# Attention blocks of a twelve-stage kernel: rounding of the maxima and division by the sums moved to GpSimd, value products half a key tile later, causal masks by matmul

## The chip, the cores and the metric

The kernel runs on one core of one Trainium2 chip. The metric is device time in microseconds (us): 3737.1 us before, the median of three runs (3736.11 to 3738.52). The engines are named as in the profile: PE (TensorE matmul), PEld (its weight load), DVE (VectorE), ACT (ScalarE), POOL (GpSimd), SP (SyncE, which issues the DMAs).

## The reference

One sequence `x` of 2048 tokens with 128 channels passes through four layers of the form feed-forward, attention, feed-forward, each added to `x` after a layer norm:

```
x = x + 0.5 * ffn_L(layernorm(x))
x = x + attn_L(layernorm(x))
x = x + 0.5 * ffn_L(layernorm(x))        # L = 0, 1, 2, 3
```

The attentions are what matters here. Each computes `softmax(q k^T * scale) v` for every head and multiplies by an output matrix. Layer 0 has 8 heads of 16 channels and is causal, with a geometric term added to the scores. Layers 1 and 2 have 16 heads of 8 channels and are not causal; layer 1 adds a bias, layer 2 turns queries and keys (rope). Layer 3 is causal with 16 heads of 64 channels and latent values. The feed-forward layers (two with routing to experts, one with quantised weights, one with ternary weights) are not touched.

## The kernel before, in words

The kernel works through twelve stages in order. While one runs, the first steps of the next are woven into it by hand (`Stage.lead`). `x` lies in SBUF as four chunks of 512 tokens (`xs`); `NC` is 4, `TC` is 4 tiles of 128 tokens a chunk, `CH` is 512.

**Attention of layers 0, 1 and 2** is written by `packed` (L1325), which calls `flash` (L974). Four heads form a group. A *block* is one group with one chunk of queries: `its` (L1441 to L1444) lists 8 blocks in layer 0 (two groups, four chunks) and 16 in each of layers 1 and 2 (four groups, four chunks, the group changing slowest). Every block is worked in two passes.

- **Pass A** (`stream_a`, `some`) finds each query's largest score. PE makes the scores of two heads, 128 queries by 512 keys each, in a PSUM pair of banks (L1071; two such pairs exist, tag `s1`), and DVE reduces the pair to two columns (L1089). In layers 1 and 2 this is 32 pairs a block. In layer 0 the pairs on the diagonal (8 a block, 64 in all) are narrower, 128, 256, 384 or 512 keys, and need the causal mask: DVE adds a strip of the mask and takes the maximum in one custom instruction for each head, with a read of its accumulator behind each (L1079 to L1087). `maxima` (L1097) then reduces the four key chunks to `mx`, negated, and `put_max` (L1551) rounds it to bf16 on DVE (`top`, L1556) and keeps the remainder beside it (L1557). A later step `put` (L1561) adds both to the queries by matmuls into the bank `pm` and ACT copies the result to `q2`, so that the scores of pass B come out with the maximum subtracted. That step falls due 2000 units of a recording clock after `maxima` (L1107).
- **Pass B** (`stream_b`) makes the scores again, transposed, 128 keys by 512 queries for each head (L1213, three single banks, tag `s2`), ACT takes the exponential (L1222) into a tile `pt`, and PE multiplies `pt` with the values (L1159) into one held bank `pv`. A key tile has four heads. In layers 1 and 2 the value products of the last key tile are issued in two halves of 256 queries, after the second and the fourth head of the current one (`values`, L1130; call at L1236). In layer 0 POOL masks the diagonal `pt` tiles (L1224).
- **The end of a block** is `finish` (L1579): ACT copies `pv` to `ov`; `normal` (L1584) transposes it on PE into a bank `po` (L1587), where every head has its result and its sum of exponentials; DVE takes the reciprocal of the sums (L1592) and multiplies (L1593) into `os`. After the last group of a query chunk, `out_a` (L1604) transposes `os` on PE (L1607), ACT copies it, and `out_b` multiplies by the output matrix (L1615) and adds to `x` (L1620).

**Attention of layer 3** (`attn3`, L1793) also uses `flash`, with two heads a block (`nh == 2`, called `halved`). Its causal mask is added in PSUM by four small bf16 matmuls for each pair, made from halves of the identity and of the mask (`half_masks`, L1021 to L1028; the halves are loaded and cast at L1010 to L1019).

**What sets the order.** Passes A and B are two generators. The loop at L1272 to L1291 advances them so that A stays about one block ahead of B, and everything that PE does in both passes is recorded in that order (`keep_in_program_order`, through `pe`). A step such as `put`, `normal`, `out_a` or `out_b` is put on a list with a due time of the recording clock (`after`, L995) and is recorded into the same order when the clock passes it. The other engines are ordered by a scheduler; the reductions of pass A have high priority, and the first one of a block is tied behind the last operation of `put_max` (`newest`, L1061, L1101). Each engine runs its own list in order, so an instruction that waits holds up those behind it.

Of the kernel before, what the change touches and what calls it, by code (L numbers as in the profile page):

```python
# [64 lines left out]
def tile_macaron(ctx: ExitStack, tc: tile.TileContext, a: dict, out: bass.AP, stages=STAGES):  # L65
# [33 lines left out]
    nc.gpsimd.memset(minus_half, -0.5)  # L99

# [873 lines left out]
    def flash(io, pool, early, its, nh, causal, scale, s1, s2, pv_mm, put_max, begin, finish, poll=None,  # L974
# [8 lines left out]
        halved = nh == 2  # L983
        clock = [0.0]
        total = [0]
# [22 lines left out]
        if halved:  # L1008

            halves = {}  # L1010
            for name in ("ident", "maskq", "maskk"):
                raw = pool().tile([P, 2, P], F32, name="halfraw", tag="halfraw", bufs=2)
                for j in range(2):
                    nc.sync.dma_start(
                        out=raw[P // 2 * j : P // 2 * (j + 1)],
                        in_=a["consts"][:, slice(*CONSTS[name])].rearrange("(b i) k -> i b k", b=2),
                    )
                halves[name] = pool().tile([P, 2, P], BF16, name="half" + name)
                nc.vector.tensor_copy(halves[name], raw)  # L1019
# [9 lines left out]

        if tiled and causal:  # L1030
            junk = pool().tile([P, CH], F32, name="junk")
            strip = pool().tile([P, CH], F32, name="strip")
            nc.gpsimd.memset(strip[:, : CH - P], 0.0)
            nc.vector.tensor_copy(strip[:, CH - P :], cs("maskq"))
# [19 lines left out]
        def some(n, turns, mp):  # L1054

            g, qc = its[n]
            nk = chunks(qc)
            for first, (r, kcs) in enumerate(turns):
                before = hook(n, kcs[0], r) if hook is not None else None
                if first == 0 and before is None:  # L1060
                    before = newest[0]  # L1061
                for kc in kcs:
                    for j0 in range(0, nh, 2):
                        ps = first_pass_bank()
                        last = causal and kc == qc
                        masked = last and not tiled
                        w = (r + 1) * P if last else CH
                        for j in range(2):
                            o = j * CH
                            lhsT, rhs = s1(n, j0 + j, r, kc)  # L1070
                            pe(nc.tensor.matmul(  # L1071
                                ps[:, o : o + w], lhsT, rhs[:, :w], start=True, stop=not masked
                            ))
                            pos[0] += w
                        if masked:
                            half_masks([ps[:, j * CH + w - P : j * CH + w] for j in range(2)], "maskq")
                        both = ps.rearrange("p (j n) -> p j n", j=2)
                        with tc.high_priority() if not waiting[0] else nullcontext():
                            if last and tiled:  # L1079
                                for j in range(2):  # L1080
                                    ins = nc.vector.tensor_tensor_reduce(
                                        junk[:, :w], both[:, j, :w], strip[:, CH - w :], 1.0, NEG,
                                        ALU.add, ALU.max, mp[:, r, j0 + j, kc : kc + 1],
                                    )
                                    if before is not None:
                                        in_order(ins, before)
                                        before = None  # L1087
                            else:
                                ins = nc.vector.tensor_reduce(  # L1089
                                    mp[:, r, j0 : j0 + 2, kc], both[:, :, :w], AX.X, ALU.max,  # L1090
                                )
                        if before is not None:
                            in_order(ins, before)
                            before = None
                        yield 2 * w if tiled else w

        def maxima(n, mp):  # L1097
            nk = chunks(its[n][1])
            mx = pool().tile([P, TC, nh], F32, name="mx", tag="mxa", bufs=3)
            nc.vector.tensor_reduce(mx, mp[:, :, :, :nk], AX.X, ALU.max, negate=True)  # L1100
            put, newest[0] = put_max(n, mx, pe)  # L1101

            def done():
                put()
                ready.add(n)

            after(2000.0, done)  # L1107
# [19 lines left out]
        def stream_b():  # L1127
            pend = [None]

            def values(half=None):  # L1130

                if pend[0] is None:
                    return
                n, kt, nt, c0, pts, pv, last_exp = pend[0]
# [13 lines left out]
                if half == 0:  # L1148
                    pend_half[0] = 1
                    if hi == CH:  # L1150
                        pend[0] = None
                        pend_half[0] = 0
                else:
                    pend[0] = None
# [22 lines left out]
            for n, (g, qc) in enumerate(its):  # L1177
# [4 lines left out]
                pv = None  # L1182
                for kt in range(nt):
# [4 lines left out]
                    if halved:  # L1188
# [11 lines left out]
                        for j in range(2):  # L1200
                            pts[j] = early.tile([P, CH], F32, name="pt", tag="pt", bufs=2 * nh + 2)
# [4 lines left out]
                    for at_j, j in enumerate(() if halved else order):  # L1206
                        if alive[0] or at_j % 2:
# [13 lines left out]
                        pt = early.tile([P, CH], F32, name="pt", tag="pt", bufs=2 * nh + 2)  # L1221
# [12 lines left out]
                        if tiled and alive[0]:  # L1234
                            if at_j % 2:
                                values(at_j // 2)  # L1236
                        elif at_j == (split_at if alive[0] else nh - 1):
                            values()
                    if pv is None:
                        pv = held("pv")  # L1240
                    pend[0] = (n, kt, nt, c0, pts, pv, ex)
                    if not alive[0]:
                        io.lead(2.3)
                if poll is not None:
                    at[1] = nt
                    if flush and n + 1 < len(its) and its[n + 1][0] != g:
                        values()
                    poll(at)
            values()
# [72 lines left out]
    def attention_scratch(early):  # L1322
        return lambda dt, name: early.tile([P, CH], dt, name=name, tag="pt", bufs=10)

    def packed(io, early, hd, causal, scale, project, w, wv, wo, bias=None, outs=True):  # L1325
# [12 lines left out]
        scratch = attention_scratch(early)  # L1338
# [212 lines left out]
        def put_max(n, mx, pe):  # L1551
            top = tops[n % 3]
            tv = top.rearrange("p a r (j s) -> p a r j s", s=span)[:, :, :, :, 3:8:4]
            for i in range(nq):
                m = mx[:, :, i * per : (i + 1) * per]
                nc.vector.tensor_copy(tv[:, i, :, :, 0], m)  # L1556
                last = nc.vector.tensor_tensor(  # L1557
                    tv[:, i, :, :, 1], m, tv[:, i, :, :, 0], ALU.subtract
                )
# [19 lines left out]
        def finish(n, pv, after, pe):  # L1579
# [4 lines left out]
            def normal():  # L1584
                ps = bank("po")
                for r in range(TC):
# [3 lines left out]
                po = ps.rearrange("p (r j m) -> p r j m", r=TC, j=4)  # L1590
                rc = room[0].tile([P, TC, 4], F32, name="rc", tag="rc", bufs=2)
                nc.vector.reciprocal(rc, po[:, :, :, hd])  # L1592
                nc.vector.tensor_tensor(  # L1593
                    os[qc][:, :, g * 4 * hd : (g + 1) * 4 * hd].rearrange(
                        "p r (j d) -> p r j d", j=4
                    ),
                    po[:, :, :, :hd],
                    rc.unsqueeze(3).to_broadcast([P, TC, 4, hd]),
                    ALU.mult,
                )  # L1600
                if g == n_groups - 1:
# [62 lines left out]
        with tc.tile_pool(name="att", bufs=1) as pool, tc.tile_pool(name="far", bufs=1) as far:  # L1664
# [11 lines left out]
            room.append(far if causal else early if outs else pool)  # L1676
# [713 lines left out]
```

## Time and profile before

| what | value |
|---|---|
| median of the timed runs | 3737.1 us |
| the profiled execution's own time | 3720.8 us |
| its span in the trace | 3719.1 us |
| busy in the span | PE 3404.5 (92%), DVE 2853.9 (77%), ACT 2025.6 (54%), POOL 817.1 (22%) |
| granted PE clock, mean | 0.95 |
| attention of layer 0 | about 178 to 447 us |
| attention of layer 1 | about 855 to 1445 us |
| attention of layer 2 | about 1745 to 2345 us |
| attention of layer 3 | the stretch up to about 3570 us |

How to read it: a share of the span is an average over stages that are bound by different things. So the profile is asked by stage: windows of time for the busy engines, then the order of time around one block. The name of an operation gives the tile that it writes and those that it reads, its shapes and its count; "idle before" is the time for which its engine stood still just before, with the engine that ended this. A busy PE is not a PE at its peak, since the ends of overlapping matmuls are modelled.

### The profile page before, as it was taken

The page shows a single profiled execution, that of the slowest core. Times are in us where ns is not written, and L with a number is a line of the kernel's source. Part 1 is how long each engine was busy: PE and PEld are TensorE (multiplying, and loading weights), DVE is VectorE, ACT ScalarE, POOL GpSimd, SP SyncE. Part 2 cuts the span into 40 slices and gives each one's busy share as a digit, 9 for nine tenths or more (in the row PEclk, how much of TensorE's full clock was granted, in tenths as well). Part 3 has the DMA queues.
Part 4 walks back from the last instruction along what each step waited for, and adds up shares of the span by engine and source line. Part 5 has one row for each costly group of instructions (what it writes and reads, how often), then busy time and mean ns, then how long its engine had stood idle before and what let it go on. Part 6 is the DMA issues. An engine that isn't in the chain of part 4 may idle for free. (4 is left out here: it accounts for less than half of the span.)

```text
span 3719.1 us, 64518 instructions
## 1 busy us (share of the span) xinstructions
PE 3404.5 (92%) x25325; PEld 1837.3 (49%) x25325; DVE 2853.9 (77%) x4729; ACT 2025.6 (54%) x3815; POOL 817.1 (22%) x816
## 2 busy tenths in 40 slices
PE   7689987989999999997999999898889999999989
PEld 5543366854333333883333333376444444445457
DVE  6588556778999995778999999544777877788852
ACT  3346722317888888333888888731333344444442
POOL 1511124000000000210000000232555445533341
PEclk9779989979999999996999999898999999999999
DMA  3420123000000000100000000012443232211010
GB/s 106 98 52 14 37 62 91 7 20 9 15 6 16 6 4 7 55 25 21 10 16 10 12 6 1 26 44 68 151 146 112 96 106 98 97 57 52 24 35 12
DMA packets 124977, 170.18 MB, mean 46 GB/s; under 512 B 25152, under 2 KB 52930, under 8 KB 124672
## 3 DMA queue, kind: packets, MB, share of 16 engines
q1 hardware_dynamic: 122112, 160.80, 13.8%
q0 software_dynamic: 2560, 5.25, 0.9%
q8 instruction: 199, 3.26, 0.4%
q14 instruction: 106, 0.87, 0.1%
HBM read 101.25 MB, written 45.87 MB: 40 GB/s over the span
## 5 line engine op out<-in xcount | busy, mean ns | idle before, releaser
L1089 DVE TENSOR_REDUCE mp<-s 128x2 f32<-128x1024 f32 (+3 forms) x1440 | 1627.7, 1183 | 80.2 <-PE s L1071 56.7
L1222 ACT ACTIVATE pt<-s 128x512 f32<-128x512 f32 (+1 forms) x2368 | 1220.5, 601 | 217.7 <-PE s L1213 165.2
L1213 PE MATMUL s<-q,km 32*128 32x512 f32 (+2 forms) x2368 | 735.0, 493 | 28.8 <-ACT pt L1222 18.6
L1159 PE MATMUL pv<-pt,v 128*32 128x256 f32 (+1 forms) x8568 | 732.2, 414 | 22.9 <-ACT ov L1582 11.2
L1071 PE MATMUL s<-km,qt 32*128 32x512 f32 (+3 forms) x2368 | 617.1, 506 | 64.9 <-DVE mp L1089 45.3
L1213 PEld LDWEIGHTS s<-q,km 32*128 32x128 f32 (+1 forms) x2368 | 323.9, 184 | 531.4 <-issue 339.5
L1202 ACT ACTIVATE pt<-s 128x512 f32<-128x512 f32 (+3 forms) x640 | 306.3, 530 | 361.3 <-PE s L1194 216.3
L143 POOL TENSOR_TENSOR rs<-rs,minus_half 128x4 f32<-128x4 f32 x56 | 57.3, 1023 | 1491.8 <-DVE rs L142 1468.1
L2071 DVE TENSOR_TENSOR sum<-sum,pt 128x512 f32<-128x512 f32 (+3 forms) x328 | 260.0, 808 | 86.9 <-ACT pt L1202 85.6
L1159 PEld LDWEIGHTS pv<-pt,v 128*32 128x32 f32 x8568 | 169.2, 108 | 317.7 <-issue 147.1
L1194 PE MATMUL s<-q,k 64*128 64x512 f32 (+3 forms) x1920 | 295.1, 400 | 14.9 <-ACT pt L1202 10.5
L1159 PE MATMUL pv<-pt,latv 128*64 128x512 f32 (+3 forms) x1280 | 307.5, 560 | 1.3 <-ACT pt L1202 1.3
L2071 POOL TENSOR_TENSOR sum<-sum,pt 128x512 f32<-128x512 f32 (+1 forms) x200 | 264.7, 1324 | 179.8 <-ACT pt L1202 176.4
L1071 PEld LDWEIGHTS s<-km,qt 32*128 32x128 f32 (+1 forms) x2368 | 236.2, 191 | 123.8 <-DVE mp L1089 82.3
L1194 PEld LDWEIGHTS s<-q,k 64*128 64x128 f32 x1920 | 159.1, 186 | 222.8 <-issue 140.5
L715 ACT ACTIVATE sg<-pg 128x1024 f32<-128x1024 f32 x72 | 74.0, 1027 | 158.2 <-PE pg L229 142.0
L1071 PE MATMUL s<-k,q 64*128 64x512 f32 (+3 forms) x640 | 131.9, 430 | 19.0 <-DVE mp L1089 18.8
L1873 DVE TENSOR_TENSOR rot<-rot,tab 128x512 f32<-128x512 f32 x128 | 87.8, 686 | 74.8 <-PE rot L229 43.3
L725 PEld LDWEIGHTS pd<-l1d,h 128*128 128x128 f32 x1152 | 139.0, 191 | 5.6
L725 PE MATMUL pd<-l1d,h 128*128 128x128 f32 x1152 | 139.8, 275 | 0.0
L717 DVE TENSOR_TENSOR h<-pu,sg 128x1024 f32<-128x1024 f32 x72 | 87.8, 1220 | 51.7 <-PE pu L229 46.5
L1888 ACT CAST h<-rot 128x512 fp32r<-128x512 f32 x64 | 39.6, 619 | 159.5 <-POOL rot L1883 159.5
(572 smaller groups left out, 4736.3 us busy)
## 6 DMA issues: line engine op xcount, KB each, us to landing
tab<-in_l3rope SPq DMA_DIRECT2D x66, 256.0 KB
q<-q SPq DMA_DIRECT2D x32, 512.0 KB
k<-k SPq DMA_DIRECT2D x32, 512.0 KB
l0e<-in_l0e SPq DMA_DIRECT2D x32, 256.0 KB
q<-h SPq DMA_DIRECT2D x32, 256.0 KB
q<-rot SPq DMA_DIRECT2D x32, 256.0 KB
k<-h SPq DMA_DIRECT2D x32, 256.0 KB
k<-rot SPq DMA_DIRECT2D x32, 256.0 KB
```

The source lines that it names most:

```text
L715: nc.scalar.activation(sg, pg, AF.Silu)
L717: nc.vector.tensor_tensor(h.rearrange("p m n -> p (m n)"), pu, sg, ALU.mult)
L725: nc.tensor.matmul(pd[:, i, :], h[:, m, i * P : (i + 1) * P], wd[:, m, :], start=m == 0, stop=m == 1,)
L1071: pe(nc.tensor.matmul(ps[:, o : o + w], lhsT, rhs[:, :w], start=True, stop=not masked))
L1089: ins = nc.vector.tensor_reduce(mp[:, r, j0 : j0 + 2, kc], both[:, :, :w], AX.X, ALU.max,)
L1159: i = pe(nc.tensor.matmul(pv[out_rows, lo:hi], lhsT, pts[j][:, lo:hi], start=kt == 0, stop=kt == nt - 1 and hi == CH))
L1194: pe(nc.tensor.matmul(outs[j][:, c0:], lhsT, rhs[:, c0:], start=i == 0, stop=i == len(terms[0]) - 1 and not diag,))
L1202: ex = nc.scalar.activation(pts[j][:, c0:], outs[j][:, c0:], AF.Exp, scale=scale)
L1213: pe(nc.tensor.matmul(ps[:, c0:], lhsT, rhs[:, c0:], start=i == 0, stop=i == len(terms) - 1 and (tiled or not diag),))
L1222: ex = nc.scalar.activation(pt[:, c0:], ps[:, c0:], AF.Exp, scale=scale)
L1873: nc.vector.tensor_tensor(t.bitcast(F32), ps, halves["tabs"][i], ALU.mult)
L2071: eng.tensor_tensor(t[:, c0:], other[:, c0:], pts[j][:, c0:], ALU.add)
```

## The change

It has four parts, the first three of which concern layers 1 and 2 alone.

1. The rounding of the maxima (`put_max`) runs on GpSimd for every block but the first of a stage, and `put` falls due 3000 instead of 2000 units after `maxima`. The first reduction of the next block is tied behind `mx` itself.
2. The division: ACT copies `po` from PSUM to a tile `ot` in SBUF, and GpSimd raises the sums to the power -1 and multiplies. The last block of a stage keeps the old way on DVE.
3. The value products are issued half a key tile later; there are 12 `pt` tiles instead of 10, and the tiles of `ov` move to another pool.
4. Layer 0: the diagonal pairs of pass A get their mask by `half_masks`, as in layer 3, and then one plain reduction for both heads. The strip and the custom instruction are gone.

The diff, cut to its core:

```
+    minus_one = const.tile([P, TC, 4], F32, name="minus_one")
+    nc.gpsimd.memset(minus_one, -1.0)
...
+        lag = tiled and not causal
+        aside = tiled and not causal
...
-        if halved:
+        if causal:
             halves = {}
-            for name in ("ident", "maskq", "maskk"):
+            for name in ("ident", "maskq", "maskk")[: 3 if halved else 2]:
...
-        if tiled and causal:
-            junk = pool().tile([P, CH], F32, name="junk")
-            strip = pool().tile([P, CH], F32, name="strip")
...
-                        masked = last and not tiled
+                        masked = last
...
-                            if last and tiled:
-                                for j in range(2):
-                                    ins = nc.vector.tensor_tensor_reduce(
-                                        junk[:, :w], both[:, j, :w], strip[:, CH - w :], 1.0, NEG,
-                                        ALU.add, ALU.max, mp[:, r, j0 + j, kc : kc + 1],
-                                    )
...
-                            else:
-                                ins = nc.vector.tensor_reduce(
-                                    mp[:, r, j0 : j0 + 2, kc], both[:, :, :w], AX.X, ALU.max,
-                                )
+                            ins = nc.vector.tensor_reduce(
+                                mp[:, r, j0 : j0 + 2, kc], both[:, :, :w], AX.X, ALU.max,
+                            )
...
-            nc.vector.tensor_reduce(mx, mp[:, :, :, :nk], AX.X, ALU.max, negate=True)
-            put, newest[0] = put_max(n, mx, pe)
+            newest[0] = nc.vector.tensor_reduce(mx, mp[:, :, :, :nk], AX.X, ALU.max, negate=True)
+            if aside and n:
+                put, _ = put_max(n, mx, pe, nc.gpsimd)
+            else:
+                put, newest[0] = put_max(n, mx, pe)
...
-            after(2000.0, done)
+            after(3000.0 if aside and n else 2000.0, done)
...
-            pend = [None]
+            pend = []
...
+                        while not alive[0] and len(pend) > 1:
+                            values()
...
                         if tiled and alive[0]:
-                            if at_j % 2:
-                                values(at_j // 2)
+                            if at_j % 2 and (not lag or at_j == nh - 1 or len(pend) > 1):
+                                values(pend_half[0] if lag else at_j // 2)
...
                     if flush and n + 1 < len(its) and its[n + 1][0] != g:
-                        values()
+                        while pend:
+                            values()
...
-        def put_max(n, mx, pe):
+        def put_max(n, mx, pe, eng=nc.vector):
...
-                nc.vector.tensor_copy(tv[:, i, :, :, 0], m)
-                last = nc.vector.tensor_tensor(
-                    tv[:, i, :, :, 1], m, tv[:, i, :, :, 0], ALU.subtract
-                )
+                eng.tensor_copy(tv[:, i, :, :, 0], m)
+                last = eng.tensor_tensor(tv[:, i, :, :, 1], m, tv[:, i, :, :, 0], ALU.subtract)
...
+                if causal or n == len(its) - 1:
...
+                else:
+                    ot = room[1].tile([P, CH], F32, name="ot", tag="ov", bufs=2)
+                    nc.scalar.copy(ot, ps)
+                    po = ot.rearrange("p (r j m) -> p r j m", r=TC, j=4)
+                    rc = room[0].tile([P, TC, 4], F32, name="rc", tag="rc", bufs=2)
+                    nc.gpsimd.tensor_tensor(rc, po[:, :, :, hd], minus_one, ALU.pow)
+                    nc.gpsimd.tensor_tensor(
+                        out, po[:, :, :, :hd],
+                        rc.unsqueeze(3).to_broadcast([P, TC, 4, hd]), ALU.mult,
+                    )
...
-            room.append(far if causal else early if outs else pool)
+            room.append(far if causal else pool)
```

## The prediction

> **What bounds the kernel now.** I read the table of 50 us windows first, to see which engine fills which stage. Its columns are the busy time (and count) of PE, PEld, DVE, ACT and POOL, the granted PE clock, the DMA share and GB/s. The first two lines are of attn0 (about 178 to 447 us), the third of attn1 (855 to 1445), the last of attn2 (1745 to 2345).
>
> ```profile
> 200.00:250.00 50.00, 45.06 (x281) 23.48 (x281) 39.35 (x103) 28.19 (x60) 9.11 (x32) 0.79 0.15 38
> 350.00:400.00 50.00, 46.90 (x411) 20.00 (x408) 44.92 (x93) 35.51 (x72) 5.59 (x17) 1.00 0.04 12
> 1100.00:1150.00 50.00, 49.19 (x509) 18.95 (x505) 49.14 (x49) 44.43 (x86) 0.00 (x0) 1.00 0.06 14
> 2000.00:2050.00 50.00, 49.19 (x509) 18.99 (x505) 49.14 (x50) 44.38 (x87) 0.00 (x0) 1.00 0.05 13
> ```
>
> In attn1 and attn2 DVE is full, POOL empty. PE looks full too, so I read the timeline of one block boundary (a block is one group of heads with one query chunk; 16 in each of these stages). Columns: start, busy time, instruction, idle before it.
>
> ```profile
> 1042.67 0.20 DVE L1556 CAST top<-mx 128x16 bf16<-128x16 f32 x1
> 1042.91 0.23 DVE L1557 TENSOR_TENSOR top<-mx,top 128x16 bf16<-128x16 f32 x1
> 1043.01 8.01 DVE L1089 TENSOR_REDUCE mp<-s 128x2 f32<-128x1024 f32 x7
> ...
> 1050.05 1.07 PE L1159 MATMUL pv<-pt,v 128*32 128x512 f32 x8 [0.47 <-ACT ov L1582]
> 1051.05 0.66 PE L1587 MATMUL po<-cst,ov 128*128 128x128 f32 x4
> 1051.64 0.50 PE L1071 MATMUL s<-km,qt 32*128 32x512 f32 x2
> 1051.74 0.26 DVE L1592 RECIPROCAL rc<-po 128x16 f32<-128x16 f32 x1 [0.72 <-PE po L1587]
> 1052.24 4.61 DVE L1089 TENSOR_REDUCE mp<-s 128x2 f32<-128x1024 f32 x4
> ```
>
> Seven reductions run back to back, 8.01/7 = 1.14 us each: DVE sets the pace. In the same stretch PE's round (four score products and four value products) takes 1.01 us where nothing holds it, so PE has about 0.13 of 1.14 to spare. But at the boundary DVE stands from 1051.02 to 1052.24 (reciprocal and multiply aside), because PE runs the wide value products and four transposes before the next first pass product, which ends at 1051.64 + 0.50 = 1052.14. The stretches belong to DVE, the boundary to PE.
>
> For attn0 the groups by form give the operation that goes, its accumulator read, and the reductions and masks (the attn3 rows of L1026) that come:
>
> ```profile
> L1081 DVE CUSTOM_DVE_ANT_0 junk<-s,strip 128x512 f32<-128x512 f32 x32 | 22.0, 689 | 3.4 <-PE s L1071 1.0 <-PE s L1213 0.8
> L1081 DVE DVE_READ_ACCUMULATOR2_ANT mp<- 128x1 f32 x128 | 10.6, 83 | 0.0
> L1089 DVE TENSOR_REDUCE mp<-s 128x2 f32<-128x256 f32 x32 | 13.1, 410 | 2.4 <-PE s L1026 2.4
> L1026 PE MATMUL s<-halfmaskq,halfident 64*128 64x128 bf16 x512 | 38.8, 228 | 0.0
> ```
>
> And POOL's rows, the nearest to what it is given:
>
> ```profile
> L143 POOL TENSOR_TENSOR rs<-rs,minus_half 128x4 f32<-128x4 f32 x56 | 57.3, 1023 | 1491.8 <-DVE rs L142 1468.1
> L222 POOL TENSOR_TENSOR wdnL<-l3d,wdnH 128x128 fp32r<-128x128 f32 x1 | 0.5, 454 | 0.0
> ```
>
> **The change, part by part**, against the profiled execution (span 3719.1, time 3720.8). The timed runs' median is 3737.1, 16 us more; I carry the difference over unchanged.
>
> 1. *Masks in attn0.* Its diagonal has 8 blocks x 8 pairs = 64 pairs. A pair was two masked maxima with accumulator reads, now one reduction. Busy, for widths 128, 256, 384, 512: 2 x (286, 423, 554, 689 + 83) = 0.74, 1.01, 1.27, 1.54 us; new 0.41, 0.68, 0.94, 1.22. That is 0.33 each, 21 us in all. PE gains four mask products a pair. In attn3 the next product starts 0.21 us after the first of four, so 64 x 0.21 = 13 us at full clock, and about 0.4 a pair where the granted clock is 0.50, as it is from 180 to 200 us. What counts is who waits. In the first two blocks (180 to 202 us) PE and ACT wait for DVE, but from 190.6 only, since PE waits there for a key DMA; at half clock a wide pair becomes bank free, products 0.8, masks 0.4, reduction 1.15 over two banks, about 1.25 us a pair against 1.58: I take -2.5 for both blocks. In the chunk 1 and 2 blocks PE waits for the old maxima (2.9 + 1.2 us in the waits of 280 to 291 alone, weight loads included): -1.1 each, four blocks, -4.5. In the chunk 3 blocks DVE never waits, but PE is 4.1 to 5.0 of 5 busy: what DVE saves, the masks take, 0. Sum **-7**. Bounds: -21 (all of DVE's saving, masks hidden) to +13 (masks alone). The four mask loads now stand on SP's queue after the second of eight y loads (these took 10.5 us of issue from 156.25); keys and queries follow at 169.5, 2.7 us after the last y load, which covers the four. Their two casts on DVE stand ahead of the first normalisation: +0.5 at most, once.
>
> 2. *Rounding of the maxima on POOL* (15 blocks in each of two stages). DVE loses cast and subtraction, 1042.67 to 1043.01 = 0.34 us in a full stretch: 30 x 0.34 = 10.2. Bounds -10 and 0. The give-back: just after, PE inserts pm (0.67) into its round, 1.68 us between two first pass products against 1.14 of DVE, and the DVE time that covered this is what goes; pm also comes right after the score products instead of after the value products, with one PSUM bank fewer. I keep 0.23 a block: **-7**. POOL's two small operations (0.2 to 0.3 each by the 128x128 row less its elements) begin when mx is ready; the built order has three PE rounds from the last product of the maxima to pm, was two, so about 1 us is left. Before the last block A's stream has ended: +0.5 once a stage.
>
> 3. *Division on POOL from ScalarE's copy.* Reciprocal and multiply, 1051.74 to 1052.24, lie inside PE's gap: the next reduction would wait until 1052.14 anyway. So taking them off DVE gives 0 to 0.1 a block. The copy (0.59, by the row of ov) starts when ACT is idle (1.17 us before 1052.16) and delays the next exponentials by 0.1 to 0.2; ACT is 44.4 of 50 busy and makes it up. Costed **0**; without that idle time, up to +0.2 x 28 = +6.
>
> 4. *The wait this adds.* In the last group of heads the output transposes read the divided sums, and the built order keeps them two rounds after po. In the old trace po starts at 1361.17 and these transposes at 1363.43: 2.26 later. New chain from po's start: po 0.7, copy 0.59, hand-over 0.1, power P, multiply 0.455, hand-overs 0.1: 1.95 + P. PE waits P - 0.3, with value products and the next first pass products queued behind it and DVE behind those; DVE already waited there 0.44 (at 1365.15), so nothing absorbs it. P: no 128x16 power was run. If POOL's excess over a plain 4 element operation (1.02 - 0.19) is fixed, 1.05; if it goes by element, 0.18 + 16 x 0.21 = 3.5. I take the geometric middle, 1.9, and both ends for the range. Three such blocks a stage, the third half covered after the first pass has ended: 5 x 1.6 = **+8** (+4 to +16). The other 22 blocks read the result much later: 0.
> The rows make POOL's multiply 454 against DVE's 291 ns, and its power at least 4 times DVE's reciprocal of 255. [...]
>
> 5. *Value products half a key tile later.* They no longer wait for the exponentials: in the waits of 900 to 1340 us PE's loads waited 50.0 us, 158 times, for those, 0.3 each. In stretches DVE hides that. At the boundary an earlier PE may shorten the gap; bounds -0.3 and 0 a block, taken -0.1: **-3**. Where the group of heads changes, one more half tile is drained in one go, 0.57 us of PE, six times, half of it covered: **+1** to +2.
>
> Sum: -7 - 7 + 0 + 8 - 3 + 1 = **-8 us**: 3712.8 in a profiled execution, 3729 as timed.
>
> **Rivals.** 0.2% is 7.5 us, about what can be told from no change.
> - *Nothing left* (0.28): DVE's small operations were cover for PE's pm and boundary work. Item 2 gives 2, item 5's 3 goes: -7 - 2 + 8 + 1 = 0, 3737. For it: the gap of 1.22 us is PE's. Against: 7 reductions without a pause after the cast.
> - *Masks bind PE in attn0* (0.17): the place is the diagonal blocks, the price 64 x 0.21 = 13 us at full clock, and it decides from where PE waits less than 0.21 a pair for DVE. +13 - 7 + 8 - 3 + 1 = +12: 3749. For it: PE's busy time at 350 to 400, the half clock at 180 to 200. Against: PE waits for L1081 in every diagonal block.
> - *The power goes by element* (0.13): P = 3.5, 5 x 3.2 = 16, with item 2 eaten to -2 and item 5 to +1: -7 - 2 + 16 + 1 = +8: 3745. It decides from P of about 3.4.
> - That the moves do not happen is excluded: the built order has 30 roundings and 30 divisions on POOL, 30 more copies on ACT.
>
> **How the numbers follow.** The forecast has 0.42, its own range 3705 to 3730. Best case -21 - 10 + 4 - 9 = -36; worst +13 + 6 + 16 + 2 = +37; neither is likely whole, and 3710 to 3752 leaves out about 2 in 10. Faster 0.42, same 0.28, slower 0.30.
>
> **What would show it.** Right: DVE's mx followed at once by the next reduction; blocks of attn1 0.2 to 0.4 us shorter; the first diagonal blocks' end before 200 us. Wrong: PE idle on POOL before the output transposes above 3.2 us; diagonal blocks of chunk 3 longer than 18 us; the boundary gap above 1.3 us; PE waiting on POOL before pm.

## The result and the profile after

The changed kernel takes 3754.1 us (median of 22 runs, 3742.7 to 3780.7) against 3736.2 us for the old one in the same rounds: a ratio of **1.0054, 95% interval 1.0042 to 1.0066**, some 20 us slower. I had forecast 8 us faster, with 0.42 for faster and 0.30 for slower. The profiled execution has a span of 3749.6 us (before: 3719.1) at a mean granted PE clock of 0.939 (0.950).

The same windows of 50 us as in the prediction, of the changed kernel, and one more, 1150 to 1200. Columns: busy time and count of PE, PEld, DVE, ACT, POOL, granted PE clock, DMA share, GB/s.

```profile
200.00:250.00 50.00, 44.87 (x366) 24.93 (x362) 42.85 (x72) 23.91 (x54) 10.12 (x33) 0.84 0.24 61
350.00:400.00 50.00, 48.25 (x449) 21.38 (x448) 42.76 (x58) 35.17 (x70) 5.57 (x17) 0.97 0.04 12
1100.00:1150.00 50.00, 49.23 (x518) 19.97 (x517) 48.70 (x46) 47.25 (x90) 4.22 (x5) 1.00 0.05 13
1150.00:1200.00 50.00, 48.73 (x385) 16.52 (x385) 39.36 (x38) 36.27 (x69) 3.83 (x4) 0.72 0.05 13
2000.00:2050.00 50.00, 49.23 (x514) 20.03 (x514) 48.55 (x45) 46.85 (x89) 4.36 (x6) 1.00 0.04 9
```

Where the clock is 1.00 the attention stages look as hoped: DVE does the same reductions in less busy time, and ACT has gone from 44.4 to 47. The line that matters is the fourth. PE is as "busy" as ever, 48.7 of 50, but it issues 385 matmuls where the old kernel issues 490 in the same window, because the clock granted to it fell to 0.72 in the mean. In the old profile the same window has 1.00.

The starts of the 16 maxima (`mx`) of each stage cut the trace into blocks. At clock 1.00 a block takes 37.9 us instead of 38.6. Some blocks, though, take 42.4, 49.5 and 43.7 us, and the last group's 45.5 to 49.1 instead of 42.8 to 45.1. So the change made most blocks shorter and a few much longer. Four stretches hold the whole span (from start to start of the instructions named, one profiled execution each; the last column is the mended kernel of the end of this document):

| stretch | before | after | mended |
|---|---|---|---|
| layer 0, first to last `mx` | 218.6 | 205.6 | 205.5 |
| layers 1 and 2, first to 13th `mx` of each | 960.3 | 966.5 | 949.2 |
| layers 1 and 2, 13th `mx` to the last copy of `oT` | 352.5 | 376.8 | 345.8 |
| all the rest | 2187.6 | 2200.6 | 2186.1 |

The rest is code that the change leaves alone, and it moves by as much between executions of kernels that are equal there (2179 to 2212 in the runs below). What the change did is in the first three rows: -13, +6, +24.

**The long blocks at a change of the group of heads.** PE's timeline of the changed kernel, from some 4 us after the ninth maximum of layer 1 (at 1162.8 us). Columns: start, busy time, instruction, idle time before it.

```profile
1166.35 1.07 PE L1156 MATMUL pv<-pt,v 128*32 128x256 f32 x16
1167.59 1.06 PE L1156 MATMUL pv<-pt,v 128*32 128x512 f32 x8 [0.17 <-ACT pt L1221]
1168.59 0.50 PE L1212 MATMUL s<-q,km 32*128 32x512 f32 x1
...
1169.87 0.50 PE L1212 MATMUL s<-q,km 32*128 32x512 f32 x1 [0.53 <-ACT pt L1221]
1170.36 0.66 PE L1585 MATMUL po<-cst,ov 128*128 128x128 f32 x4
...
1171.34 1.15 PE L1212 MATMUL s<-q,km 32*128 32x512 f32 x2
...
1172.32 0.79 PE L1212 MATMUL s<-q,km 32*128 32x512 f32 x1
1173.04 1.94 PE L1156 MATMUL pv<-pt,v 128*32 128x512 f32 x8
```

Here all value products in arrears are drained (24 in one go), and then the lag leaves a stretch without any, from 1168.65 to 1173.04. A score product of 512 columns takes 0.50 us at 1169.87 and 0.79 at 1172.32: the clock has fallen in between. The windows around it, whole engines:

```profile
1165.10:1168.60 3.50, 3.33 (x44) 1.08 (x44) 2.58 (x3) 1.99 (x4) 0.00 (x0) 1.00 0.23 61
1168.60:1172.00 3.40, 2.87 (x23) 1.45 (x19) 3.06 (x4) 3.27 (x7) 0.16 (x1) 1.00 0.22 58
1172.00:1202.70 30.70, 30.45 (x200) 8.60 (x197) 21.27 (x18) 19.02 (x36) 3.15 (x2) 0.50 0.00 1
1202.70:1233.40 30.70, 29.93 (x317) 11.82 (x317) 29.09 (x28) 28.37 (x55) 3.83 (x4) 1.00 0.03 8
```

At 0.50 the stage gets through 17 reductions of pass A in 30.7 us, at 1.00 through 26 (the counts above hold DVE's other work too): about 9 x 1.13 = 10 us lost in this one drop. The trace's clock record changes only at points 3.41 us apart. I call the time between two of them a step. The drop begins at one of these points, 1172.0, and the step that ends there holds only 0.1 us of value products. The old kernel, same change of group, whose drain is one half tile shorter and whose next value products come 3.1 us after it:

```profile
1163.04 1.07 PE L1159 MATMUL pv<-pt,v 128*32 128x512 f32 x8 [0.41 <-ACT pt L1222]
1164.04 0.50 PE L1213 MATMUL s<-q,km 32*128 32x512 f32 x1
...
1167.20 1.06 PE L1159 MATMUL pv<-pt,v 128*32 128x512 f32 x8
```

**The long blocks of the last group.** PE, then POOL, around an output transposition of the changed kernel:

```profile
1377.68 0.49 PE L1212 MATMUL s<-q,km 32*128 32x512 f32 x1
1380.64 1.12 PE L1614 MATMUL oT<-cst,o 128*128 128x128 f32 x4 [2.48 <-POOL o L1604]
1381.69 1.08 PE L1156 MATMUL pv<-pt,v 128*32 128x256 f32 x8
```

```profile
1377.20 2.91 POOL L1603 TENSOR_TENSOR rc<-ot,minus_one 128x16 f32<-128x16 f32 x1 [9.87 <-ACT ot L1600]
1380.18 0.41 POOL L1604 TENSOR_TENSOR o<-ot,rc 128x128 f32<-128x128 f32 x1
```

PE stands 2.48 us for POOL's power and product, and the value products behind the transposes stand with it: they start at 1381.69, though the last exponential ahead of them had ended at 1379.09. The transposes take 1.12 us for 0.66, the value products 1.08 for 0.64: the clock has dropped here too, to 0.50 from 1380.2 to 1387.0. The groups by form give POOL's prices (count, busy time, mean ns):

```profile
L1603 POOL TENSOR_TENSOR rc<-ot,minus_one 128x16 f32<-128x16 f32 x30 | 87.1, 2905 | 283.4 <-ACT ot L1600 283.4
L145 POOL TENSOR_TENSOR rs<-rs,minus_half 128x4 f32<-128x4 f32 x56 | 57.4, 1025 | 431.2 <-DVE rs L144 407.7 <-DVE wsum L693 23.3
L1604 POOL TENSOR_TENSOR o<-ot,rc 128x128 f32<-128x128 f32 x30 | 12.2, 406 | 2.4
```

### The profile page after: what moved, and what is told of

Read it like the earlier page. It is cut to its first block, busy times and chain, and to the rows that moved or that the text cites. A ratio compares the mean times of both kernels' runs of the same rounds, so it can differ in the third digit from the quotient of the medians.

```text
span 3749.6 us, 64471 instructions
## 1 busy us (share of the span) xinstructions
PE 3431.4 (92%) x25581; PEld 1872.3 (50%) x25581; DVE 2815.8 (75%) x4418; ACT 2060.6 (55%) x3845; POOL 932.1 (25%) x936
## 5 line engine op out<-in xcount | busy, mean ns | idle before, releaser
L1079 DVE TENSOR_REDUCE mp<-s 128x2 f32<-128x1024 f32 (+1 forms) x1504 | 1675.8, 1166 | 144.2 <-PE s L1071 65.8
L1221 ACT ACTIVATE pt<-s 128x512 f32<-128x512 f32 (+1 forms) x2368 | 1240.0, 599 | 175.9 <-PE s L1212 121.6
L1212 PE MATMUL s<-q,km 32*128 32x512 f32 (+2 forms) x2368 | 752.1, 501 | 25.7 <-ACT pt L1221 15.8
L1156 PE MATMUL pv<-pt,v 128*32 128x256 f32 (+1 forms) x8568 | 745.7, 421 | 20.1 <-ACT ov L1580 10.8
L1212 PEld LDWEIGHTS s<-q,km 32*128 32x128 f32 (+1 forms) x2368 | 336.6, 187 | 540.9 <-ACT pt L1221 373.6
L1556 POOL CAST top<-mx 128x16 bf16<-128x16 f32 x30 | 7.6, 255 | 750.6 <-PE s L1212 419.3
L145 POOL TENSOR_TENSOR rs<-rs,minus_half 128x4 f32<-128x4 f32 x56 | 57.4, 1025 | 431.2 <-DVE rs L144 407.7
L1603 POOL TENSOR_TENSOR rc<-ot,minus_one 128x16 f32<-128x16 f32 x30 | 87.1, 2905 | 283.4 <-ACT ot L1600 283.4
```

Source lines behind the costliest of these rows:

```text
L1079: ins = nc.vector.tensor_reduce(mp[:, r, j0 : j0 + 2, kc], both[:, :, :w], AX.X, ALU.max,)
L1156: i = pe(nc.tensor.matmul(pv[out_rows, lo:hi], lhsT, pts[j][:, lo:hi], start=kt == 0, stop=kt == nt - 1 and hi == CH))
L1212: pe(nc.tensor.matmul(ps[:, c0:], lhsT, rhs[:, c0:], start=i == 0, stop=i == len(terms) - 1 and (tiled or not diag),))
L1221: ex = nc.scalar.activation(pt[:, c0:], ps[:, c0:], AF.Exp, scale=scale)
L1603: nc.gpsimd.tensor_tensor(rc, po[:, :, :, hd], minus_one, ALU.pow)
```

## The experiments

All were timed in five rounds against the old kernel on the same chip, so each ratio is to the old kernel timed beside it. Three theories stood at first. **Clock**: PE's granted clock falls to half where PE stands, or runs score products alone, for most of a 3.4 us step; the lag makes such a stretch at changes of the group (1168.65 to 1173.04 above), and POOL's division one at the output transposes (2.48 us above). **Wait**: the waits on POOL alone. **ScalarE**: the copies of `po` (ACT 44.4 to 47 of 50) make ACT the bound of every block.

### Undoing one thing at a time

`x1_late_out`:

```
-                    after(OUT_A if causal else 1500.0, out_a)
+                    after(OUT_A if causal else 6500.0, out_a)
```

> The changed kernel with one number changed: the output transposes fall due 6500 instead of 1500 units after the division was begun, so that GpSimd's power (2.9 us) and product have ended when PE comes to them. Clock theory (PE's granted clock falls to 0.5 where PE stands, or issues score products alone, for most of a step of 3.4 us): the waits of the four last blocks of each stage go and with them the drops at 1380, 1428 and 1469 us; 16 to 20 us less than the changed kernel, ratio to before about 1.000; the drops 9 us after the maxima at changes of the group of heads stay. Wait theory (the wait on GpSimd alone, five times 2.6 us): 13 us less, ratio 1.002. ScalarE theory (the copies of po make ScalarE the bound of every block): no gain, 1.004 to 1.006.

Measured 0.9979 (0.9956 to 1.0002), 0.0075 below the changed kernel. The waits on POOL and the drops behind them are gone: the 13th `mx` to the last copy of `oT` takes 357.6 instead of 376.8 us, 19 less, though group drops of 24 and 10 us now fall into that stretch (one of 3.4 us in the changed kernel). That is more than the 13 us of the wait theory. Four of six changes of the group still drop (24, 31, 10 and 10 us long).

`x2_no_lag`:

```
-        lag = tiled and not causal
+        lag = False
```

> The changed kernel without the lag: the value products are issued where the old kernel issues them; masks, rounding, division and the 12 exponential tiles stay. Clock theory: the drops 9 us after the maxima at changes of the group (42.4, 49.5 and 43.7 us blocks) go, 10 to 20 us; blocks at full clock get longer, from 37.9 towards 38.4, if the lag is what shortened them, 0 to 10 us back; the waits at the output transposes stay. Ratio 1.000 to 1.004. ScalarE theory: ScalarE is loaded as before and PE waits for exponentials again on top: 1.006 to 1.009.

Measured 1.0027 (1.0013 to 1.0040). No change of the group drops; the waits and drops at the transposes stay. Blocks at full clock take 38.9 us, longer than the old 38.6, so the lag had given 1.0 a block here.

`x3_div_dve`:

```
-                if causal or n == len(its) - 1:
+                if True:
```

> The changed kernel with the division back on VectorE from PSUM, so without ScalarE's copy of po and without GpSimd's power. Clock theory: the waits at the output transposes and the drops there go, 16 to 20 us less; the drops at changes of the group stay; blocks at full clock 37.9 to 38.2. Ratio 1.000 to 1.002. ScalarE theory: blocks get shorter in all of both stages, and ratio is 0.997 or less. If both were wrong and the division on GpSimd brought the shorter blocks: 38.6 us blocks and 1.004.

Measured 1.0020 (0.9998 to 1.0042), at the upper end, with group drops of 10, 10 and 41 us in its profile. Its full clock blocks take 37.9 us, the same as with the division on POOL. That ends the ScalarE theory: without the copy nothing gets shorter. The division moved to POOL buys nothing.

`x4_dummy` adds work: after the first key tile of a new group,

```
+                    if extra[0] and keep_busy is not None:
+                        extra[0] = False
+                        keep_busy(n, 2, pe)
...
+        def keep_busy(n, k, pe):
+            ps = bank("oT")
+            for i in range(k):
+                pe(nc.tensor.matmul(
+                    ps, masks_b["ident_r"], km[its[n][0], 0][:, 0, :], start=True, stop=True
+                ))
```

> The changed kernel with work added: at each change of the group (6 in all) PE issues two products of 128x128 by 512 whose result is read by nobody, after the four scores of the new group's first key tile, where the lag leaves a stretch of over 4 us without value products. Clock theory: the granted clock stays 1.00 there, the blocks of 42.4, 49.5 and 43.7 us become 38.5 to 39.5, and the kernel is 8 to 18 us faster than the changed one in spite of 12 more products (ratio 1.000 to 1.003). ScalarE theory and wait theory: 12 products of 0.35 us are only added: 1.005 to 1.007, and the drops, if they are random, stay.

Measured **0.9995 (0.9981 to 1.0009)**, 0.0059 or some 22 us below the changed kernel, with more work. All six changes of the group stay at clock 1.00, and those blocks take 39.2 us. The drops at the output transposes stay.

### One part alone

`x5_masks_only` is the changed kernel with `lag = False`, `aside = False` and the division on DVE: only layer 0's masks remain (and the 12 tiles and the new pool of `ov`).

> Of the change only the masks of layer 0 (and the 12 exponential tiles): rounding, division and value products as in the old kernel. My term 1 (-7): ratio 0.998, first to last maximum of layer 0 some 205 to 208 us, blocks of layers 1 and 2 as before, 38.6 us. If the masks bind PE (my second rival): ratio 1.002 or more. If all of what layer 0 seemed to gain was the clock of that one execution: 1.000.

Measured **0.9962 (0.9949 to 0.9975)**, -14 us. Not all of that is the masks'. In the profile layer 0 takes 207.8 us from first to last `mx` instead of 218.6: -10.8, inside the 205 to 208 expected. Another 8.3 us lie in the first blocks of layers 1 and 2 (51.9 to 46.4 and 52.6 to 49.8 us), where there are no masks; by the code, the 12 tiles and the pool of `ov` are what differs there. In the old kernel ACT waits in these two blocks 6.3 and 6.4 us, 8 times each, for value products that still read a `pt` tile; in `x5_masks_only` this wait is gone. With the lag it is back (5.1 and 6.4 us in `x7_masks_lag` below), and the first blocks are nearly as long as before (50.6 and 52.7). Read from these waits, the 12 tiles are worth some 8 us here, and the lag takes them again. PE is busy for 237.2 us from 182 to 441 us (before, 178 to 447: 237.1), so the 256 added products did not lengthen its work; the mean clock there is 0.94 instead of 0.90.

`x6_masks_round` adds the rounding on POOL (`aside` on); `x12_round_early` is the same with the step `put` due as in the old kernel:

```
-            after(3000.0 if aside and n else 2000.0, done)
+            after(2000.0, done)
```

> Masks and the rounding of the maxima on GpSimd; division and value products as in the old kernel. My term 2 (-7): full clock blocks of layers 1 and 2 of 38.3 to 38.4 us and a ratio 0.002 below the run with masks alone. The kernel without the lag had 38.9 us: if the rounding (with its later pm) is what costs there, blocks of 38.8 to 38.9 and a ratio 0.001 to 0.002 above the run with masks alone; if it was the division's copy on ScalarE, 38.4 to 38.6.

> Masks and rounding on GpSimd, with the step that adds the maxima due 2000 instead of 3000 units after them; division and value products as in the old kernel. With 3000 the blocks were 38.8 us against 38.55 with masks alone. If the place of that step (one round later, right after score products) is what lengthened them: 38.2 to 38.4 us and a ratio of 0.994 to 0.995, my term 2 as predicted. If VectorE isn't what sets the end there at all: 38.5 to 38.6 and the ratio of masks alone, 0.996. If PE waits there for GpSimd's two operations (0.25 and 0.27 us and hand-overs): 38.6 to 38.9.

Measured 0.9966 (0.9954 to 0.9978) and 0.9946 (0.9928 to 0.9963); blocks of 38.8 and 38.5 us, against 38.55 with masks alone. DVE of the first, then of the second, from a maximum on:

```profile
1068.57 3.48 DVE L1079 TENSOR_REDUCE mp<-s 128x2 f32<-128x1024 f32 x3
1072.36 4.62 DVE L1079 TENSOR_REDUCE mp<-s 128x2 f32<-128x1024 f32 x4 [0.32 <-PE s L1212]
```

```profile
1104.83 8.24 DVE L1079 TENSOR_REDUCE mp<-s 128x2 f32<-128x1024 f32 x7
1113.94 0.26 DVE L1594 RECIPROCAL rc<-po 128x16 f32<-128x16 f32 x1 [0.86 <-PE po L1585]
```

With the late step DVE stands in the middle of the stretch, since PE puts `pm` in just after score products. With the early one it runs seven reductions through and stands 0.86 us at the boundary (0.72 in the old kernel). Either way what DVE is relieved of is waited for a few us later. By the starts of the reductions in a full clock block of `x12_round_early`: the first one follows the start of the maximum after 0.14 us instead of 0.59 (-0.45), then 0.24 is lost where `pm` comes in, 0.13 at the boundary and 0.07 at the end. Its ratio lies 0.0016 below that of masks alone, in the range that I had set for a gain, but the two intervals overlap and the blocks show none of it: from the first to the 13th `mx` layers 1 and 2 take 951.8 us in both.

`x7_masks_lag` is masks and lag, rounding and division on DVE.

> Masks and the lag; rounding and division on VectorE as in the old kernel. If the lag alone shortens the blocks: 37.9 to 38.1 us at full clock, against 38.6; if it needs VectorE relieved of the rounding: 38.2 to 38.5. Clock theory: drops to 0.5 some 9 us after the maxima at some of the six changes of the group of heads, none at the output transposes; ratio 0.996 to 1.001 by how many there are and how long.

Measured 0.9996 (0.9974 to 1.0018), with four group drops of 14 to 44 us. Full clock blocks take 37.9 us: the lag alone gives what the whole change gives. One line each of the old kernel and of this run, the DVE stretch from the division to the next maximum:

```profile
1052.24 28.73 DVE L1089 TENSOR_REDUCE mp<-s 128x2 f32<-128x1024 f32 x25
```

```profile
1097.68 27.23 DVE L1079 TENSOR_REDUCE mp<-s 128x2 f32<-128x1024 f32 x24
```

28.73/25 = 1.149 us each, 27.23/24 = 1.135. Start to start the first is 1.13 at the beginning and 1.14 and 1.16 in turn later. So DVE wasn't quite full in the old kernel. Over a full clock block the lag gives 0.31 us in the stretches (30 x 0.0103) and 0.36 at the boundary, where two reductions start 2.08 us apart instead of 2.44. Between 900 and 1290 us the weight loads of the value products waited for exponentials 139 times, 43.6 us in all, in the old kernel, and twice, 1.0 us, in this run. That these waits of PE were what spaced the reductions is read from this; no run changes them alone.

### Mending the two places

`x8_late_fresh` has the late output transposes, and after a change of the group the first tile's value products as early as the old kernel's:

```
+                            if kt and fresh[0]:
+                                if at_j == 1:
+                                    values(0)
+                                    fresh[0] = False
-                            if at_j % 2 and (not lag or at_j == nh - 1 or len(pend) > 1):
+                            elif at_j % 2 and (not lag or at_j == nh - 1 or len(pend) > 1):
```

> The changed kernel mended in the two places: the output transposes due 6500 units after the division, and after each change of the group the value products of the first key tile issued at once, after two scores of the second tile, as the old kernel does, and the lag taken up again from there. Clock theory: no drop at the six changes of the group nor at the output transposes, full clock blocks of 37.9, ratio to before 0.992 to 0.995. If the drops come from something else than the stretch without value products, they stay at some changes of the group and the ratio is that of the run with late transposes alone, 0.998.

Measured 0.9917 (0.9892 to 0.9942). One of six changes of the group still dropped, for 10 us: there the 3.1 us without value products, 999.65 to 1002.76, fell just inside a step of the clock, which held 0.3 us of them.

`x9_late_dummy` has the late transposes and the two unread products.

> The changed kernel with both mends of the first runs: output transposes due 6500 units after the division, and two products that nobody reads at each change of the group (added work). Clock theory: no drop of the granted clock at any of the six changes of the group, none at the output transposes; ratio to before 0.991 to 0.994, and the first group change of layer 1, which still dropped in the run with the value products issued at once, stays at 1.00.

Measured **0.9902 (0.9884 to 0.9920)**, the fastest: 1% faster than the old kernel, 1.5% faster than the changed one. No drop at any of the places. PE at the change of group that had dropped for 30.7 us, and the window after it:

```profile
1150.54 0.66 PE L1590 MATMUL po<-cst,ov 128*128 128x128 f32 x4
1151.03 0.73 PE L1640 MATMUL oT<-km,ident_r 128*128 128x512 f32 x2
...
1153.31 1.07 PE L1156 MATMUL pv<-pt,v 128*32 128x512 f32 x8
```

```profile
1143.00:1183.00 40.00, 38.35 (x390) 15.64 (x387) 37.78 (x36) 36.02 (x68) 4.16 (x6) 1.00 0.04 11
```

With 0.73 us of filler the clock is 1.00 through these 40 us; the value products 1.5 us later take 1.07 us, not 1.94.

`x10_lag_dummy` is masks, lag and the filler, with nothing moved to POOL.

> Masks, lag and the two unread products at each change of the group (added work), with rounding and division left on VectorE: nothing moved to GpSimd, no copy of po, no wait to mend. If the two moves to GpSimd buy little (blocks 38.0 with the lag alone, 37.9 with the rounding aside as well): ratio 0.991 to 0.995, within 0.001 to 0.002 of the run with both mends. If they buy what my prediction said (0.23 a block and more): 0.002 to 0.003 above it.

Measured 0.9921 (0.9904 to 0.9937); spans of 3686.0 and 3686.7 us in the two profiles. The ratios differ by 0.0019 and their intervals overlap: that the moves to POOL give anything isn't shown.

`x11_busy_wait` leaves the waits on POOL and fills them:

```
+                ps = bank("po")
+                for i in range(6 if not causal else 0):
+                    pe(nc.tensor.matmul(
+                        ps, masks_b["ident_r"], km[g, 0][:, 0, :], start=True, stop=True
+                    ))
```

> The changed kernel with added work and the wait on GpSimd left as it is: ahead of each output transposition PE issues six products of 0.34 us that nobody reads, 2.0 us in all, which fit into its wait of some 2.6 us. Clock theory: the drops to 0.5 at the output transposes (five of five in the changed kernel) go, though the wait stays; the four last group blocks, 48.2, 45.5, 49.1 and 47.6 us, get 1 to 2 us shorter each, ratio 1.002 to 1.005, drops at changes of the group stay. If the drops were not from PE's standing but from the queue behind the wait: they stay, and the ratio is 1.005 to 1.008.

Measured 1.0008 (0.9991 to 1.0024), lower than the 1.002 to 1.005 that I had expected.

```profile
1367.20 1.66 PE L1614 MATMUL po<-km,ident_r 128*128 128x512 f32 x6
1369.67 0.66 PE L1619 MATMUL oT<-cst,o 128*128 128x128 f32 x4 [0.81 <-POOL o L1604]
1370.26 0.64 PE L1156 MATMUL pv<-pt,v 128*32 128x256 f32 x8
```

PE still stands for POOL, 0.81 us after the 1.66 us of filler, yet the transposes take 0.66 and not 1.12 us: the clock held, at 1.00 from 1369.4 to 1376.2. The last two blocks of both stages take 46.4, 45.3, 46.7 and 42.9 us, against 49.1, 47.6, 48.2 and 45.5 in the changed kernel and 42.9, 43.4, 43.3 and 40.2 with late transposes. So of 20.6 us lost in these four, 9.1 are the clock's (a little more, as the fillers cost something) and 11.5 the wait's.

### The drops counted

Over all profiles, drops to 0.50 that begin within 15 us after the fifth, ninth and thirteenth `mx` of layers 1 and 2, where pass B changes the group (six places in each profile):

| kernels | drops |
|---|---|
| lag, nothing added (after, x1, x3, x7, x11) | 19 of 30 |
| no lag (before, x2, x5, x6, x12) | 0 of 30 |
| lag with the old spacing after the drain (x8) | 1 of 6 |
| lag with filler (x4, x9, x10) | 2 of 18, of 3.4 us each |

Which of these places drop goes with how the stretch without value products (3.1 us without the lag and in x8, 4.1 to 4.7 with the lag alone) falls on the steps of the clock. Take for each place the step with the least time of value products. In the first three rows 17 places have a step with 0.32 us or less, and all 17 dropped; of the other 49, with 0.35 us or more, 3 dropped (at 0.40, 0.88 and 0.90 us). In the last row 17 of the 18 places have a step with 0.24 us or less, and 2 dropped: so it is the filler and not a shift against the steps that holds the clock there.

And at the first three output transposes of each stage, where the changed kernel's PE stands for POOL (six places): 17 of 18 where it stands (after, x2, x4), 0 of 6 where it waits as well but the wait is filled (x11), 0 of 60 where POOL has ended by then or isn't used (the other ten profiles). A drop of 3.4 to 10.2 us that begins 3 to 6 us after the 15th or 16th `mx` of a stage stands in 12 of the 14 profiles, the old kernel's included; it isn't the change's and is not counted.

## Why the prediction was wrong

The steps that failed are 2, 4 and 5, and behind 4 and 5 stands one thing that no step had: **the granted clock was taken as given**. I multiplied instructions by their old durations at full clock, and never asked what a stretch with little PE work does to the clock behind it.

- *Step 1, masks, -7 taken.* Mechanism right, size too small: -8 to -13 by the profiles (layer 0 takes 205.5 to 210.8 us in the 13 kernels that have the masks, 218.6 in the one old profile). The -14 of `x5_masks_only` holds the tiles' 8 us as well, which no step of mine had and which the changed kernel doesn't keep. The two blocks of chunk 3 came out as priced: 41.0 to 39.8 and 44.4 to 45.1 us (x5, all at clock 1.00), about 0. The excess lies in chunks 1 and 2, -9.5 instead of -4.5 in x5, where the old profile has clocks of 0.73 to 0.91 and the new one 0.79 to 1.00. That is in the nature of my working: I priced the waits that go, and left the clock as it was. How much of it is chance of one execution isn't settled. The second rival (masks bind PE) fell.
- *Step 2, rounding, -7 taken.* Wrong. The sign I looked for is there (in the changed kernel `mx` ends and the next reduction starts at once, 1086.19 to 1086.32), but it is worth nothing: +0.25 a block without the lag, 0 with the early step, 0 with the lag (37.9 in x3 and x7). The seven reductions that I quoted, 8.01 us, belong to the first dozen of a block, the only ones that follow at DVE's own 1.13 us. I read the pace of 32 reductions from these; the line of 25 quoted above stood in the same trace. My first rival had it right here: DVE's small operations were cover for PE's work.
- *Step 3, division, 0 taken.* Right as to blocks: 37.9 with and without.
- *Step 4, the wait, +8 taken.* P is 2.9 us, not 1.9. From the two sizes in the trace I estimate (2905 - 1025)/12 = 157 ns for each element and some 400 fixed. (The 0.18 and 0.19 that I set for a plain operation lie on the line through the old profile's POOL products on 128x128 and 128x512, 454 and 1278 ns.) PE waits 2.5 us on average, six times, not 1.6 five times: +15 instead of +8. At five of the six waits the clock drops for 3.4 to 6.8 us, which adds some 9 us in four blocks. In all +24 in the third row of the table, although the lag shortens that stretch too. (Two counts of the prediction are off, without weight in its sum: 30 less 6 leaves 24 other blocks and not 22, and ACT makes 30 copies and not 28.) The third rival had the right reason and asked for 3.4 us; with the clock 2.9 was enough.
- *Step 5, lag, -3 taken; drain, +1 to +2.* "In stretches DVE hides that" is the sentence that failed: the lag gives 0.31 us a block there and 0.36 at the boundary, where I took 0.1 in all. The gain was some four times mis-sized: -11 over the first three groups of both stages (960.3 to 949.2 in the mended kernel, fillers included). The loss was ten times mis-sized: the drain and the empty stretch behind it cost some 17 us in the changed kernel's profile (966.5 against 949.2), 22 by the timed ratios of x4 and after, almost all by the clock.

By the stretches of the profiles the sum is -13 + 0 + 0 + 24 - 11 + 17 to 22 = +17 to +22, against 18 (medians) to 20 (ratio) measured. Each is one execution, so it is no closer than some us; but the two mends together take 0.0152 off the ratio, and singly 0.0075 and 0.0059.

None of my warning signs showed: the longest wait before an output transposition was 2.7 us (I had said 3.2), the diagonal stretches of chunk 3 took 14.3 and 16.8 us (18), the boundary gap was 1.16 us (1.3), and PE never waited on POOL before `pm`. Two signs of being right did show, in a kernel that was slower: the reduction at once after `mx`, and blocks some 0.65 us shorter. The first diagonal blocks ended late (`mx` at 203.9 and 213.2 us, before at 192.1 and 202.0), but they began 11 us late as well, so that sign can't be read. No sign looked at the clock column, which stands in the very windows that I showed.

PE's idle time alone does not tell when the clock falls or comes back. From 1168.60 to 1172.00 PE is busy 2.87 of 3.40 us by the record and stands 0.53 at the longest, and the clock falls; from 1172.00 to 1202.70 it is busy 30.45 of 30.70 and the clock stays down for nine steps of 3.41 us. At the output transposes PE stands 2.45 to 2.71 us, six times. In the steps ahead of the five drops it is busy 0.92 to 2.35 us; in the two steps around the wait without a drop (1475.8 to 1482.6) it is busy 2.25 and 1.84 us, less than in the step from 1168.60, and the clock stays at 1.00.

What of PE's work the clock counts isn't settled. In the steps ahead of 17 of the 20 unfilled group drops there are 0 to 0.32 us of value products (128 rows), beside score products of 32 rows, four side by side (at 1168.59 to 1168.60 four start); but three drops follow steps with 0.40, 0.88 and 0.90 us. Why one drop lasts 3.4 us and another 44 isn't settled either. Whether the filler works by its size of 128x128 or just by filling 0.73 us was not tried.

## What to carry to other kernels

Before moving or delaying work on TensorE, look at the granted clock beside the busy time, and ask of each drain, wait or delay what it leaves PE to do. Here, without filler, all 17 places that had a step of 3.41 us with 0.32 us or less of value products dropped, and the price was not the gap but the stretch at half clock behind it, 3 to 44 us. Read an engine's pace from the whole of a block, not from the stretch where it catches up: DVE set the pace here for a third of a block, and what it was relieved of was waited for in the rest. And where a kernel gains in most blocks and loses in a few, time per block (here by the starts of one small instruction) finds both in one view; two unread products and one later due time turned +0.5% into -1.0%.

## What the runs showed of the hardware

- The granted clock of PE fell to 0.50 after a step in which PE was recorded as 84% busy (2.87 of 3.40 us), and stayed there for 3.4 to 44 us in the attention stages, in steps of 3.41 us; in the drop of 30.7 us PE was recorded as busy for 30.45 us. The length differs from place to place (10.2, 30.7 and 3.4 us at three changes of group of one execution).
- Two products of 128x128 by 512, 0.73 us in all, stood at 18 places, and at 16 of them the clock stayed at 1.00; without them, with the same lag, at 11 of 30.
- GpSimd's power on 128x16 took 2905 ns, on 128x4 1025; its product on 128x128 406 (DVE 291); its cast and subtraction on 128x16 255 and 269 (DVE 236 and 232).
